# Norms by pairs of blocks behind the experts, a table loaded ahead, and products that nobody reads

## The chip, the cores and the metric

The kernel runs on one core of one Trainium2 chip. The core has five engines with queues of their own: TensorE (PE, with PEld for its weight loads), VectorE (DVE), ScalarE (ACT), GpSimd (POOL) and SyncE (SP, which here only issues DMAs). The metric is the device time of one execution in microseconds (us); a run gives one such time, and a median of several is compared. All numbers are float32.

## The reference

A two-layer perceiver: 16 sets of 64 tokens of 256 features (`x`, 1024 tokens, here 8 blocks of 128) read a memory `ctx` of 16 x 1601 rows. Six steps follow each other, each added to `x` after a layer norm:

```python
x = x + L0_xattn(_layernorm(x), ctx, top_k=32, ...)   # the 32 best of 1601 memory rows
x = x + L0_attn(_layernorm(x), ...)                   # retention with a decay
x = x + L0_ffn(_layernorm(x), ...)                    # attention over sets, then 8 experts
x = x + L1_xattn(_layernorm(x), ctx, ctx, ...)        # 16 heads over the whole memory
x = x + L1_attn(_layernorm(x), ...)                   # random features
x = x + L1_ffn(_layernorm(x), ...)                    # three trees of leaves, then attention
```

The places that matter here are the first norm with its queries, and the end of the third step with the norm that opens the fourth:

```python
def _ln(x, g, b, eps=1e-05):
    mu = jnp.mean(x, -1, keepdims=True)
    v = jnp.mean((x - mu) ** 2, -1, keepdims=True)
    return (x - mu) * jax.lax.rsqrt(v + eps) * g + b
# L0_ffn: each token goes to one expert, y is its gated output
y2 = _ln(y1 + moe(y1), ln2_g, ln2_b)
x = x + y2
# L1_xattn begins
qn = layernorm(_layernorm(x), norm_w, norm_b)
Q = qn @ Wq + bq
```

## The kernel before

`X` (128 partitions, 8 blocks, 256 features) stays on the core for the whole kernel. The blocks are handled in two halves of four. The program is written with tiles and a planner that puts the instructions of all engines in an order by modelled readiness and priority. Stages written under `manual_schedule` keep the written order on PE, DVE and ACT; the other queues (POOL, SP) are still ordered by the planner, and instructions outside such a stage are fitted in where the planner sees room. On each engine the order is then fixed: an instruction that waits holds up all behind it.

**The start (L475 to L490).** `normed_half(0)` takes the statistics of four blocks on DVE (`moments`, L152), a root on ACT (L160), a reciprocal (L161) and four normalised blocks `xn` (L280). `turned_half` turns them with PE transposes (L290) and copies them out by ACT and DVE (L293). `normed_half(1)` follows for the other half, then a small `power` activation that brings ACT the table of Exp (L479), then `queries(0)`: eight 128x512 products recorded at L211, which need the weights `w_x` from memory. The second half is turned, `query_keys(0)` makes the keys' side of the scores (L211 again, then L307), and `turned_and_scored` turns the first pair of memory tiles (L327) and scores them (L340). SP issues `X`, the first memory pair (L243, L246), then `rows` (L485) and further pairs; POOL issues `w_x`, `cols` and `w_mha`.

**The way back from the experts (L1179 to L1241).** Eight experts run one after the other on PE (L1098, L1112, L1115); ACT copies each result out (`ye`, L1117) and stores it to `done` in memory. While the results come back, PE and ACT also work on the memory of the next stage (values L632 and L640, turns L589 and L594): this filler is written earlier in the program with a lower priority, so the planner puts it where it finds room. `returned(k)` gathers block `k` of the results by an indirect DMA on POOL (L1182), adds it to `y1` with its gate (L1186), takes mean and variance (L1190, L1191), and leaves the centred, scaled block in `xa` (L1192). `root` is an activation with the square root on ACT (L1207) and a reciprocal on DVE (L1208). `summed(k)` adds the normed block to `X` (L1198) and takes the statistics of the sum (L1202, L1203). From these come `off` (L1223) and the normed queries `qn` (even blocks on DVE at L1233, odd ones on ACT at L1228). `turned_queries(0)` transposes them (L193, written out by ACT at L1155), and `head_pairs` makes the queries of all heads (L1165, L1173), after a `power` activation with Exp (L1238).

The order written before: an activation `root` on the constant `eps` (L1215), four `returned`, one root for the four, four `summed`, one root for the four, `off`, four `qn`, then the transposes; the second half's four `returned` come at the very end. `root` at L1215 depends only on `eps`; in the profiled execution it ran at 7.34 us, far ahead of its stage.

**What follows (L1696).** A loop over 16 sets, 4 parts and 2 column blocks: scores (`sc`, L1569), their maximum (`nmax`, L1582), exponents (L1590), transposes (L1604) and products with the values (L1624). In its first eight units a generator, `second_half`, finishes the second half: a root by Newton steps on POOL (`inverse_root`, L548 to L560), `summed` (L1198), POOL's `qn` (L1275), and `added` (L1252, L1259).

PSUM comes in pools with tags; tiles of one tag take turns: 5 buffers of tag `mm` at the start, 4 on the way back.

Of the kernel before, what the change touches and what calls it, by code (L numbers as in the profile page):

```python
# [10 lines left out]
F32 = mybir.dt.float32  # L11
I32 = mybir.dt.int32
AF = mybir.ActivationFunctionType
ALU = mybir.AluOpType
# [3 lines left out]
P = 128  # L18
D = 256
# [28 lines left out]
EPS = 1e-5  # L48
# [28 lines left out]
def perceiver_kernel(  # L77
# [178 lines left out]
    with ExitStack() as ph:  # L256
# [15 lines left out]
        qbk = act.tile([P, NB], F32, name="qbk", tag="qbk")  # L272
        qkTs = []

        def normed_half(half):
            xn = act.tile([P, NB // 2, D], F32, name="xn", tag=f"a{half}")
            k0, n = HALVES[half]
            mv, rstd = moments(X, k0, n)
            for k in range(n):
                nc.vector.tensor_scalar(  # L280
                    xn[:, k, :], X[:, k0 + k, :], mv[:, k, 0:1], rstd[:, k : k + 1],
                    ALU.subtract, ALU.mult,
                )
            return xn

        def turned_half(half, xn, copies):
            for c in range(2):
                pt = ps_m.tile([P, 512], F32, name="ps_t", tag="mm")
                for j in range(4):
                    nc.tensor.transpose(  # L290
                        pt[:, j * P : (j + 1) * P], xn[:, j, c * P : (c + 1) * P], ident
                    )
                copies[c](out=xnT[:, c, half * 512 : (half + 1) * 512], in_=pt)  # L293
# [179 lines left out]


        with tc.manual_schedule(engines=order):  # L475
            xn = normed_half(0)
            turned_half(0, xn, (nc.scalar.copy, nc.vector.tensor_copy))
            xn = normed_half(1)
            nc.scalar.activation(small.tile([P, 1], F32, name="power"), eps, AF.Exp)  # L479
            queries(0)  # L480
            turned_half(1, xn, (nc.vector.tensor_copy, nc.vector.tensor_copy))
            query_keys(0)
            mems = {0: pair(0)}
            sco = turned_and_scored(0, mems[0], nothing, nothing)
            nc.sync.dma_start(out=rows, in_=rows_in.partition_broadcast(P))  # L485
            mems[1] = pair(1)
            last = iter(())
            nc.gpsimd.tensor_tensor(
                X, X, row("L0_xattn_bo").unsqueeze(1).to_broadcast([P, NB, D]), ALU.add
            )  # L490
            for k in range(NB):
                chosen = []
                choice = choose(sco, chosen)
                next(last, None)
                next(choice)
                if k == 0:
                    queries(1)
                    query_keys(1)
                next(choice)
                next(last, None)  # L500
                next(choice)

                def between():
                    next(last, None)

                def behind():
                    next(choice, None)

                if k + 2 < NB:
                    mems[k + 2] = pair(k + 2)  # L510
                if k + 1 < NB:
                    sco = turned_and_scored(k + 1, mems[k + 1], between, behind)
                else:


                    cT = act.tile([P, 2, NT], F32, name="cT", tag="c")
                    taken = act.tile([P, NB // 2, D], F32, name="taken", tag="a0")
                    outputs(
                        0, lambda k, ps: nc.scalar.copy(taken[:, k : k + 2, :], ps), between
                    )  # L520
                    behind()
                    nc.vector.tensor_tensor(X[:, 0:4, :], X[:, 0:4, :], taken, ALU.add)
                last = gather(k, mems.pop(k), *chosen, k == NB - 2)
            for _ in last:
                pass
            outputs(1, lambda k, ps: nc.vector.tensor_tensor(
                X[:, k : k + 2, :], X[:, k : k + 2, :], ps, ALU.add
            ))
# [254 lines left out]
    with ExitStack() as ph:  # L783
# [395 lines left out]
        def returned(k, mv, dst):  # L1179

            back = qn[:, k, :]
            nc.gpsimd.indirect_dma_start(  # L1182
                out=back, out_offset=None, in_=done,
                in_offset=bass.IndirectOffsetOnAxis(ap=from_row[:, k : k + 1], axis=0),
            )
            nc.vector.scalar_tensor_tensor(  # L1186
                y1[:, k, :], back, gval[:, k : k + 1], y1[:, k, :], ALU.mult, ALU.add
            )
            st = small.tile([P, 6], F32, name="b_st", tag="b_st", bufs=2)
            nc.vector.bn_stats(out=st, in_=y1[:, k, :])  # L1190
            nc.vector.bn_aggr(out=mv, in_=st)  # L1191
            nc.vector.scalar_tensor_tensor(  # L1192
                dst, y1[:, k, :], mv[:, 0:1], row("ln2_g"), ALU.subtract, ALU.mult
            )
# [7 lines left out]
            nc.vector.bn_stats(out=st, in_=X[:, k, :])  # L1202
            nc.vector.bn_aggr(out=mv, in_=st)  # L1203

        def root(mv, scale, bias):
            rstd = small.tile([P, 4], F32, name="b_rstd", tag="b_rstd", bufs=2)
            nc.scalar.activation(rstd, mv[:, :, 1], AF.Sqrt, bias=bias, scale=scale)  # L1207
            nc.vector.reciprocal(rstd, rstd)  # L1208
            return rstd

        mvs = [small.tile([P, 4, 2], F32, name="b_mv", tag=f"b_mv{i}", bufs=1) for i in range(3)]
        with tc.manual_schedule(engines=order):
            nc.scalar.activation(small.tile([P, 1], F32, name="root"), eps, AF.Sqrt)  # L1215
            for k in range(4):
                returned(k, mvs[0][:, k, :], xa[:, k, :])
            rstd = root(mvs[0], 1.0, eps)
            for k in range(4):
                summed(k, xa[:, k, :], rstd[:, k : k + 1], mvs[1][:, k, :])  # L1220
            rstd = root(mvs[1], 1.0 + EPS, eps2)
            off = small.tile([P, 4], F32, name="b_off", tag="b_off", bufs=1)
            nc.vector.scalar_tensor_tensor(  # L1223
                off, mvs[1][:, :, 0], -1.0, rstd, ALU.mult, ALU.mult
            )
            for k in range(4):
                if k % 2:
                    nc.scalar.activation(  # L1228
                        qn[:, k, :], X[:, k, :], AF.Identity,
                        bias=off[:, k : k + 1], scale=rstd[:, k : k + 1],  # L1230
                    )
                else:
                    nc.vector.tensor_scalar(  # L1233
                        qn[:, k, :], X[:, k, :], mvs[1][:, k, 0:1], rstd[:, k : k + 1],
                        ALU.subtract, ALU.mult,
                    )
            turned_queries(0)
            nc.scalar.activation(small.tile([P, 1], F32, name="power"), eps, AF.Exp)  # L1238
            for oc in range(2):
                head_pairs(oc, 0)  # L1240
            for k in range(4, NB):  # L1241
                returned(k, mvs[2][:, k - 4, :], place[:, k - 4, :])
# [839 lines left out]
```

## Time and profile before

| what | value |
|---|---|
| median of 3 runs | 1519.57 us (1512.68 to 1520.9) |
| the profiled execution: its own time | 1511.88 us |
| its span | 1509.8 us |
| PE busy | 1457.7 us (97%), 10966 products |
| PEld / DVE / ACT / POOL busy | 65% / 66% / 52% / 21% |
| mean granted clock of TensorE | 0.992 |
| chain that ended last | PE 86%, DVE 7%, DMA 2%, issue 2%, POOL 1%, ACT 1% |

The span runs from the first to the last instruction that the profiler saw; the execution's own time has 2.1 us around it. "Busy" is time in which an engine's instructions ran; a busy PE is not PE at its peak, since products are pipelined and one f32 product leaves more than one record. The chain that ended last is followed back from the last instruction, at each step to what released it. The granted clock is the share of TensorE's full speed that it was allowed in a window. In a timeline the number in brackets is the idle time before a group and what ended it.

### The profile page before, as it was taken

Reading aid. Unit: us, or ns where it says so; the run is one execution under the profiler, and the core shown is the slowest. Engines: PE = TensorE matmul, PEld = TensorE weight load, DVE = VectorE, ACT = ScalarE, POOL = GpSimd, SP = SyncE. Lnnn points to the kernel's source line nnn. Section 1 sums busy time; section 2 is a strip of 40 time slices with the busy share of each in tenths; the row PEclk is TensorE's granted clock in tenths of the full one; section 3 lists DMA queues with packets and bytes.
Section 4 is the critical chain, followed back from the end, with each engine's and each line's share of the span. In section 5 each row is a group of like instructions: output and inputs, shape, how many; then the busy total and the mean of one; then the engine's idle time right before and its main releaser. Section 6 shows DMA issues by size and latency. Waiting matters only on the chain.

```text
span 1509.8 us, 28072 instructions
## 1 busy us (share of the span) xinstructions
PE 1457.7 (97%) x10966; PEld 988.6 (65%) x10966; DVE 995.2 (66%) x2111; ACT 788.3 (52%) x1983; POOL 320.3 (21%) x788
## 2 busy tenths in 40 slices
PE   7999988999979999999999999999999998999999
PEld 4666646677846777777777777777777665446445
DVE  2888858861268877877787787778776666523322
ACT  4666523341056666666666666666666565321221
POOL 2000007211032223132212313231240322231000
PEclk9999999999989999999999999999999999999999
DMA  9455132035621011011011101101110120100000
GB/s 327 144 168 168 37 115 72 1 126 181 221 76 45 3 45 47 4 46 45 11 39 45 46 3 47 45 15 35 45 45 3 45 88 10 37 1 0 0 14 14
DMA packets 76596, 92.85 MB, mean 62 GB/s; under 512 B 2584, under 2 KB 71760, under 8 KB 76336
## 3 DMA queue, kind: packets, MB, share of 16 engines
q1 hardware_dynamic: 72912, 82.82, 17.2%
q0 software_dynamic: 2400, 7.20, 1.9%
q8 instruction: 86, 1.41, 0.4%
q10 hardware_dynamic: 1152, 1.05, 0.2%
q14 instruction: 46, 0.38, 0.1%
HBM read 85.82 MB, written 5.24 MB: 60 GB/s over the span
## 4 chain that ended last, share of the span: by engine, by line
PE 86%; DVE 7%; DMA 2%; issue 2%; POOL 1%; ACT 1%; SPq 0%; DVEq 0%; POOLq 0%; ACTq 0%
PE ps_v L632 12%; PE ps_k L610 11%; PE pt L1604 9%; PE sc L1569 7%; PE po L1624 7%; PE ps_h L1834 5%; PE ps_o L1856 4%; PE pt L327 3%; PE sc L340 3%; DVE nmax L1582 3%; PE pu L412 3%; PE pt L589 3%; PE ps_p L211 2%; PE ps_h L1098 2%; PE ps_v L1868 2%; PE ps_y L1112 2%
## 5 line engine op out<-in xcount | busy, mean ns | idle before, releaser
L1590 ACT ACTIVATE a<-sc,nmax 128x384 f32<-128x384 f32 (+2 forms) x512 | 304.4, 600 | 162.8 <-DVE nmax L1582 162.8
L1582 DVE TENSOR_REDUCE nmax<-sc 128x1 f32<-128x384 f32 (+2 forms) x512 | 258.2, 567 | 97.0 <-PE sc L1569 96.9
L1604 PEld LDWEIGHTS pt<-ident,a 128*128 128x128 f32 (+1 forms) x1664 | 189.3, 141 | 47.2 <-issue 26.7
L1612 DVE COPY aT<-pt 128x512 f32<-128x512 f32 (+1 forms) x288 | 191.4, 686 | 34.5 <-PE pt L1604 26.3
L632 PE MATMUL ps_v<-w_x,mT 128*128 128x256 f32 (+1 forms) x832 | 202.6, 382 | 2.9 <-ACT kT L618 1.0
L610 PE MATMUL ps_k<-mT,w_x 128*128 128x384 f32 (+2 forms) x512 | 204.7, 523 | 0.5 <-ACT kT L618 0.5
L1604 PE MATMUL pt<-ident,a 128*128 128x128 f32 (+1 forms) x1664 | 204.6, 274 | 0.0
L632 PEld LDWEIGHTS ps_v<-w_x,mT 128*128 128x128 f32 (+1 forms) x832 | 145.6, 186 | 25.4 <-DVE aT L1612 5.1
L610 PEld LDWEIGHTS ps_k<-mT,w_x 128*128 128x128 f32 x512 | 87.0, 189 | 103.9 <-issue 72.1
L1569 PE MATMUL sc<-kT,qh 32*128 32x384 f32 (+2 forms) x1024 | 124.1, 547 | 0.0
L1624 PE MATMUL po<-aT,v 128*32 128x128 f32 (+1 forms) x3328 | 118.3, 277 | 6.0 <-DVE aT L1612 6.0
L594 ACT ACTIVATE mT<-pt,cols 128x384 f32<-128x384 f32 (+2 forms) x128 | 87.0, 683 | 63.2 <-PE pt L589 62.3
L576 POOL TENSOR_SCALAR memt<-memt,m_nmean,m_rstd 128x256 f32<-128x256 f32 (+1 forms) x208 | 113.0, 560 | 1.7
L1590 ACT ACTIVATION_READ_ACCUMULATOR a<-sc,nmax 128x1 f32 x512 | 105.9, 207 | 0.0
L1624 PEld LDWEIGHTS po<-aT,v 128*32 128x32 f32 (+1 forms) x3328 | 82.5, 109 | 31.6 <-issue 14.2
L618 ACT ACTIVATE kT<-ps_k,cols 128x384 f32<-128x384 f32 (+2 forms) x128 | 75.9, 594 | 35.4 <-PE ps_k L610 34.5
L570 DVE BATCH_NORM_STATS2 m_st<-memt 128x6 f32<-128x256 f32 (+1 forms) x208 | 83.7, 403 | 6.9 <-DMA memt<-in_mem_dram 6.6
L640 DVE COPY v<-ps_v 128x512 f32<-128x512 f32 (+1 forms) x112 | 64.9, 580 | 35.3 <-PE po L1624 28.0
L1609 ACT COPY aT<-pt 128x512 f32<-128x512 f32 x128 | 75.6, 591 | 0.7 <-PE pt L1604 0.7
L1823 DVE SCALAR_TENSOR_TENSOR hT<-leafb,memt,hT 128x512 f32<-128x512 f32 x48 | 35.2, 747 | 57.2 <-ACT hT L1841 57.2
L589 PE MATMUL pt<-ident,memt 128*128 128x128 f32 (+1 forms) x416 | 67.1, 273 | 5.7 <-ACT mT L594 1.7
L1841 ACT ACTIVATE hT<-ps_h,cols 128x512 f32<-128x512 f32 x48 | 33.0, 687 | 74.9 <-PE ps_h L1834 74.9
(369 smaller groups left out, 2000.8 us busy)
## 6 DMA issues: line engine op xcount, KB each, us to landing
memt<-in_mem_dram SPq DMA_DIRECT2D x32, 1536.0 KB
w<-in_moe_w_dram SPq DMA_DIRECT2D x16, 1024.0 KB
memt<-in_mem_dram SPq DMA_DIRECT2D x32, 65.0 KB
w_x<-in_w_x_dram POOLq DMA_DIRECT2D x2, 1024.0 KB
mT<-in_fff_w_dram SPq DMA_DIRECT2D x2, 1024.0 KB
kT<-in_fff_w_dram SPq DMA_DIRECT2D x2, 1024.0 KB
rows<-in_rows_dram SPq DMA_DIRECT2D x1, 1430.5 KB
X<-in_x_dram SPq DMA_DIRECT2D x2, 512.0 KB
```

What stands on the lines that cost most here:

```text
L570: nc.vector.bn_stats(out=st[0:m, c, :], in_=mt[0:m, c, :])
L576: nc.gpsimd.tensor_scalar(mt[0:m, c, :], mt[0:m, c, :], nmean[0:m, c : c + 1], rstd[0:m, c : c + 1], ALU.add, ALU.mult,)
L589: nc.tensor.transpose(pt[:, j * P : j * P + chunk(c)], mt[0 : chunk(c), c, dc * P : (dc + 1) * P], ident[0 : chunk(c), 0 : chunk(c)],)
L594: nc.scalar.activation(mT[:, dc, c0 * P : c0 * P + n], pt[:, 0:n], AF.Identity, bias=col("L1_norm_b", dc), scale=col("L1_norm_w", dc),)
L610: nc.tensor.matmul(ps[:, 0:n], lhsT=wk[:, dc, oc * P : (oc + 1) * P], rhs=mT[:, dc, n0 : n0 + n], start=(dc == 0), stop=(dc == 1),)
L632: nc.tensor.matmul(ps[0 : chunk(c), j, :], lhsT=mT[:, dc, c * P : c * P + chunk(c)], rhs=wv[:, dc, :], start=(dc == 0), stop=(dc == 1),)
L1569: nc.tensor.matmul(scs[j][:, 0:n], lhsT=qh[rs, oc, b, :, :], rhs=kT[rs, oc, c0 * P : c0 * P + n], start=True, stop=True,)
L1582: nc.vector.reduce_max(out=nm, in_=sc[:, 0:n], axis=AX.X, negate=True)
L1590: nc.scalar.activation(aj[:, 0:n], sc[:, 0:n], AF.Exp, bias=nm, accum_out=tot[:, blk, part : part + 1])
L1604: nc.tensor.transpose(pt[0:m, j * P : (j + 1) * P], a[j][:, c * P : c * P + m], ident)
L1612: nc.vector.tensor_copy(aT[0:m, :], pt[0:m, :])
L1624: nc.tensor.matmul(po[32 * j : 32 * j + 32, :], lhsT=v[0:m, c0 + c, blk * 32 : (blk + 1) * 32], rhs=aTs[c][0:m, j * P : (j + 1) * P], star ...
```

## The change

At the start two groups of products of the identity with itself are issued on PE, 16 ahead of everything and 8 between the first half's transposes and the queries. They write a PSUM tile that nobody reads. On the way back the first half's four blocks go by pairs: the first pair's root is taken while the third block comes back, the second norm's root of the first pair while the fourth does, and the third and fourth blocks are summed after the first pair's queries are normed. Each root is now an activation of two columns, and its reciprocal stands where its result is used. The activation `root` at the head of the stage reads `even` (written on DVE at L1132 to L1134, at the end of the experts) in place of `eps`. Eight products of the identity with the fourth returned block, 128x256 each, go to PE ahead of the transposes; nobody reads them either.

```diff
+        def awake(n):
+            ps = ps_m.tile([P, P], F32, name="ps_w", tag="mm")
+            for _ in range(n):
+                nc.tensor.matmul(ps, lhsT=ident, rhs=ident, start=True, stop=True)
...
         with tc.manual_schedule(engines=order):
+            awake(16)
             xn = normed_half(0)
             turned_half(0, xn, (nc.scalar.copy, nc.vector.tensor_copy))
+            awake(8)
             xn = normed_half(1)
...
-        def root(mv, scale, bias):
-            rstd = small.tile([P, 4], F32, name="b_rstd", tag="b_rstd", bufs=2)
+        def root(mv, scale, bias, i):
+            rstd = small.tile([P, 2], F32, name="b_rstd", tag=f"b_rstd{i}", bufs=2)
             nc.scalar.activation(rstd, mv[:, :, 1], AF.Sqrt, bias=bias, scale=scale)
+            return rstd
+
+        def normed_pair(k, rstd):
             nc.vector.reciprocal(rstd, rstd)
-            return rstd
+            off = small.tile([P, 2], F32, name="b_off", tag="b_off", bufs=2)
+            nc.vector.scalar_tensor_tensor(
+                off, mvs[1][:, k : k + 2, 0], -1.0, rstd, ALU.mult, ALU.mult
+            )
+            nc.vector.tensor_scalar(
+                qn[:, k, :], X[:, k, :], mvs[1][:, k, 0:1], rstd[:, 0:1],
+                ALU.subtract, ALU.mult,
+            )
+            nc.scalar.activation(
+                qn[:, k + 1, :], X[:, k + 1, :], AF.Identity,
+                bias=off[:, 1:2], scale=rstd[:, 1:2],
+            )
...
         with tc.manual_schedule(engines=order):
-            nc.scalar.activation(small.tile([P, 1], F32, name="root"), eps, AF.Sqrt)
-            for k in range(4):
-                returned(k, mvs[0][:, k, :], xa[:, k, :])
-            rstd = root(mvs[0], 1.0, eps)
-            for k in range(4):
-                summed(k, xa[:, k, :], rstd[:, k : k + 1], mvs[1][:, k, :])
-            rstd = root(mvs[1], 1.0 + EPS, eps2)
...
+            nc.scalar.activation(small.tile([P, 1], F32, name="root"), even, AF.Sqrt)
+
+            returned(0, mvs[0][:, 0, :], xa[:, 0, :])
+            returned(1, mvs[0][:, 1, :], xa[:, 1, :])
+            first = root(mvs[0][:, 0:2, :], 1.0, eps, 0)
+            returned(2, mvs[0][:, 2, :], xa[:, 2, :])
+            nc.vector.reciprocal(first, first)
+            for k in range(2):
+                summed(k, xa[:, k, :], first[:, k : k + 1], mvs[1][:, k, :])
+            second = root(mvs[1][:, 0:2, :], 1.0 + EPS, eps2, 1)
+            returned(3, mvs[0][:, 3, :], xa[:, 3, :])
+            ps = ps_m.tile([P, D], F32, name="ps_w", tag="mm")
+            for _ in range(8):
+                nc.tensor.matmul(ps, lhsT=ident, rhs=xa[:, 3, :], start=True, stop=True)
+            first = root(mvs[0][:, 2:4, :], 1.0, eps, 0)
+            normed_pair(0, second)
+            nc.vector.reciprocal(first, first)
+            for k in range(2, 4):
+                summed(k, xa[:, k, :], first[:, k - 2 : k - 1], mvs[1][:, k, :])
+            second = root(mvs[1][:, 2:4, :], 1.0 + EPS, eps2, 1)
+            normed_pair(2, second)
             turned_queries(0)
```

More of the change, by code (lines that the diff above doesn't have):

```diff
@@ L1222, in perceiver_kernel @@
[L1222 to L1236, printed above, removed]
+            nc.scalar.activation(small.tile([P, 1], F32, name="root"), even, AF.Sqrt)
```

## The prediction

> **What bounds the kernel now.** I read the share of each engine first (PE 97%, DVE 66%, ACT 52%), then the chain of waits that ended last (PE 86%, DVE 7%), in order of time at the two places that the change touches, then the windows of the granted clock there. The chain at the start:
>
> ```profile
> 1.63 10.38 DMA w_x<-in_w_x_dram
> 12.02 0.14 issue
> 12.15 6.20 PE ps_p L211 x8
> 18.34 0.87 PE ps_t L290 x8
> 19.22 3.44 PE ps_p L211 x8
> 22.66 1.68 PE ps_b L307 x16
> 24.33 3.55 PE pt L327 x32
> ```
>
> Columns: start, length, what. From 12.15 us on TensorE never waits, so what it loses is lost at the end. Two groups of eight 128x512 products (L211) are alike, and the first takes 6.20 us, the second 3.44: until 17.2 us each record takes 0.85 us, then 0.43. The chain on the way back from the experts:
>
> ```profile
> 430.10 0.67 ACT mT L594
> ...
> 430.79 1.28 ACT L1207
> 432.09 0.31 ACT b_rstd L1207
> ...
> 436.98 0.31 ACT b_rstd L1207
> ...
> 438.19 2.04 PE ps_t L193 x8
> 440.25 5.50 PE ps_q L1165 x8
> 445.75 1.11 PE sc L1569 x8
> 446.86 2.47 DVE nmax L1582 x4
> 449.32 0.41 DVE X L1198
> ```
>
> The fourth block's variance is ready at 428.99 us, but ScalarE is in an evacuation of `mT` and must then load the square root's table (1.28 us): VectorE idles 2.85 us (429.57 to 432.42). Then come four blocks in a row on VectorE, a second root, and PE at half speed: L193 takes 0.255 us a transpose (0.115 at full clock: L327, 32 in 3.69 us), L1165 0.85 us a record at first. The clock, in windows of 3.41 us (PE busy, PEld, DVE, ACT, POOL, then granted clock):
>
> ```profile
> 351.70:355.12 3.42, 3.42 (x17) 3.14 (x16) 1.25 (x2) 0.64 (x2) 0.00 (x0) 0.51 0.00 0
> 355.12:358.53 3.41, 3.41 (x30) 3.36 (x30) 1.02 (x2) 0.00 (x0) 0.00 (x0) 0.99 0.00 0
> 426.80:430.21 3.41, 1.56 (x10) 0.85 (x9) 2.59 (x7) 1.18 (x3) 2.65 (x3) 1.00 0.41 109
> 430.21:433.62 3.41, 1.12 (x4) 0.72 (x4) 1.10 (x4) 3.38 (x5) 0.00 (x0) 0.51 0.31 68
> 437.04:440.45 3.41, 2.24 (x9) 1.59 (x10) 2.96 (x9) 2.28 (x5) 0.00 (x0) 0.50 0.39 123
> 440.45:443.86 3.41, 3.41 (x5) 1.35 (x6) 3.17 (x10) 2.09 (x3) 0.00 (x0) 0.50 0.01 2
> 443.86:447.28 3.42, 3.42 (x15) 1.38 (x14) 1.36 (x4) 2.89 (x4) 2.11 (x10) 0.99 0.02 5
> ```
>
> All changes of the clock in this execution fall on one grid of 3.41 us. A window with PE 46% busy (1.56 us) is followed by half clock, one with 63% (2.15 us, at 1235.75) is not; from half clock a full window lifts it, one with 66% (2.24 us) does not.
>
> **The start: unread products.** `ident` is ready at 1.47 us, TensorE's first real work at 8.24 us, so `awake(16)` has 6.7 us of idle time. A 128x128 f32 product leaves two records (L1098: 16 products, 32 records in 3.84 us, 0.12 each at full clock), so 32 records, about 0.24 each at half clock (L193's 0.255 the nearest row). They fill the window to 6.96 us; by then some 22 are done, the other 10 take 1.2 us: end at 8.1, before the first `xn` is out (8.09 + wait = 8.24). With other grids they end by 8.9, and the transposes, now 0.115 each, still end by 9.8. `awake(8)` is 16 records, 9.75 to 11.6, under the wait for `w_x` (12.02 us). The windows 6.96 to 10.37 and 10.37 to 13.79 then hold some 2.4 and 2.8 us, above the 2.15 that held the clock. So the first L211 group costs 3.44 instead of 6.20. What is late next: the second half's `xn`, at 15.3 us before, 0.5 earlier now, since VectorE's copy at 10.48 waited for the slow transposes; PE needs it at 15.59. ScalarE's `qT` copies end at 15.3 and 16.55, keys start at 16.46 and need the second only 0.86 us later. L327 would start at 12.15 + 3.44 + 0.87 + 3.44 + 1.68 = 21.6 instead of 24.33: **2.7 us**. Its cover is thin: the second tile of the first memory pair is needed at 22.5. `rows` (1430.5 KB) stands behind it on SP's queue and had landed at 25.91; at 418 GB/s, the most in any 2 us there, it takes 3.5 us, so the pair was there by 22.4. Bounds: 0 (it lands only at 24.33, where the trace proves it) to 2.8.
>
> [...]
>
> **The way back.** *Table.* The root's first use moves from L1215's cheap place at 7.34 us (0.19 us, off the chain) to behind `even`, which is written at 413.77 to 414.24. ScalarE then idles 7.48 us until the last `ye` copy (417.21), which hides 1.28 + 0.20; without that cover 1.48 would go before the last expert's store. No Exp stands between there and the roots, so the load at 430.79 goes.
>
> *VectorE by pairs.* A returned block costs 1.60 us, a summed one 1.06, a reciprocal or `off` 0.21, a `qn` block 0.33. From 423.05: blocks 0 to 2 end at 427.84. The first root's data are there at 425.81, its 0.30 us lies under block 2. Reciprocal and two sums: 430.2. The second root lies under block 3, which ends at 431.8 (its gather stays fourth on POOL, issued 424.04, landing 2.83 later like the first, so 426.9; all eight gathers leave POOL by 430.1 as before). Reciprocal, `off`, `qn` 0: 432.6; the third root was ready under block 3. Reciprocal and two sums: 434.95. The fourth root isn't hidden: 0.36. Reciprocal, `off`, `qn` 2: 436.1, where block 4 starts; before, 438.38. So 2.85 of idling leaves, three more small instructions (0.63) come, 2.3 remain. Block 7's variance then is ready at 442.0, POOL's root (4.43 us, 444.43 to 448.86 before) done at 446.6.
>
> *PE.* The 8 unread products of 128x256 are 16 records (L632: 32 in 7.17 us, 0.22), waiting for `xa` 3 at 431.8. The clock has fallen by then (430.21), so at 0.43: unless 82% busy lifts it at 433.62, it rises at 437.04 after 12 records, the rest end at 437.9. Queued behind them: the transposes, whose input is ready at 436.3, so 1.6 us are given back; L193 then takes 0.95 instead of 2.04, L1165 3.44 instead of 5.50. ScalarE: two `qnT` to 440.1, Exp's table and `power` to 441.6, two `qh` to 443.1. The first scores start there instead of 445.68; `nmax` ends at 446.75. That meets POOL's root: summed block 4 (L1198) starts at 446.75 instead of 449.24, **2.5 us**, and from there all follows in the old order. If the clock rises at 433.62, scores come at 441.1, but POOL's root still ends at 446.6: nothing more. If it never rises, 443.9 and 0.8 us less. Bounds: -1.0 (first rival) to 2.9 (all idling gone).
>
> **Sum.** 2.7 + 2.5 = 5.2 us. The profiled execution took 1511.88 us (span 1509.8, 2.1 around it): 1506.7. It and the fastest run (1512.68) lie 8 us below the other two (1519.57, 1520.9); nothing in the page tells why, though the grid's phase differs from run to run at most by some us. I put the gain on the middle of the four, 1516.1, and predict **1511 us**.
>
> **Rivals.**
> 1. *ScalarE's queue hides no root.* The four waiting evacuations (L594) are interleaved with roots by the planner. If the first root stands behind the one at 430.10, which itself waits for PE, the reciprocal comes at 431.15 instead of 427.84, 3.3 us late, and the way back loses 1.0. For it: the old first root stood exactly there. Against: its data come 3.2 us earlier, when only three evacuations are done. 2.7 - 1.0 = 1.7: 1514.4. Chance 0.15.
> 2. *Transposes don't hold the clock.* Window 6.96 to 10.37 then counts 1.4 us (42%, under the 46% that fell): half clock at 10.37, `awake(8)` ends at 12.6, the clock is back at 13.79, and the start gains 1.7, not 2.7: 1512.0. Against: 64.98 to 68.40 is 2.96 us transposes of 3.42 and stayed at 1.00; 351.70 to 355.12 has 1.97 us of them and lifted. [...] 0.05.
> 3. *First memory pair late.* Start gains nothing: 2.5, 1513.6. 0.10.
> 4. *Slower: the unread products don't lift the clock.* Products of one identity may not count as work like others. Then `awake(8)` runs 10.4 to 14.1, past 12.15, and the first queries end 0.75 later than now; on the way back 16 x 0.43 end at 438.7, the transposes 0.6 later. Together +1.35: 1517.5. It decides from the point where 32 products leave the clock at half at 8.24. Against: busy share alone explains every window above. 0.08.
> 5. *More than forecast*: the two half-clock windows that cost most elsewhere (187.87 and 464.34 lead into them, up to 1.7 us each) fall away as the work shifts: 8.6, 1507.5. 0.10.
>
> **How the numbers follow.** Forecast 0.52. The range 1502.5 to 1518.5 takes the sum on the lower pair of executions with rival 5 below (1512 - 8.6 = 1503.4) and the sum of rival 1 on the upper pair (1520 - 1.7 = 1518.3). 0.5%, 7.6 us, is about what a measurement of this kernel can tell from no change. 1511 against 1519.57 is 0.56%, but the new median may fall in the lower pair (1507, 0.8%) or the upper (1515, 0.3%), the former likelier if the phase of the clock made the upper one: within the forecast 0.6 to 0.4; rival 5 is mostly faster, rivals 1 to 3 a third, rival 4 same or slower. Together faster 0.50, same 0.40, slower 0.10.
>
> **What would show it.** Right: L211's first group near 3.5 us, L327 at 21.6, no idle before it from `memt`; no table load at the first root, one near 414; VectorE idle under 0.5 us in all from 423 to the second summed pair; L1165 near 3.5; summed block 4 some 5 us earlier than 449.3. Wrong: L211 still at 0.85 a record, a root that waits behind L594, or `pt` L327 waiting for a DMA. The prediction falls if the end moves by less than 2 us or more than 9.

## The result and the profile after

The changed kernel took 1509.71 us (median of 21 runs, 1505.43 to 1516.35), the kernel before 1520.52 us beside it (21 runs, 1511.95 to 1521.59). The ratio on record is 0.9945, with a 95% interval of 0.9931 to 0.9958; it is not the quotient of the two medians, which is 0.993. The profiled execution took 1505.43 us, span 1503.6, mean granted clock 0.995, 6.45 us less than the one profiled before.

The times of both kernels fall into two groups. Before: 4 runs at 1512 and 17 from 1518.6 to 1521.6. After: 19 from 1505.4 to 1511.0 and 2 at 1515.5 and 1516.4. The gain in the median therefore has two parts: within the short group some 3.6 us (medians 1512.2 and 1508.6; both profiles belong to it), and a shift from the long group to the short one. The start and the way back can be read in the two profiles. The second part needed experiments of its own.

The start, TensorE's timeline of the changed kernel. Columns: start, length, engine, line, what, and in brackets the idle time before it with what ended it.

```profile
1.53 6.39 PE L280 MATMUL ps_w<-ident 128*128 128x128 f32 x32 [1.53 <-POOL eps L135]
...
9.85 1.95 PE L280 MATMUL ps_w<-ident 128*128 128x128 f32 x16
12.21 3.67 PE L211 MATMUL ps_p<-xnT,w_x 128*128 128x512 f32 x8 [0.41 <-DMA w_x<-in_w_x_dram]
...
16.59 3.60 PE L211 MATMUL ps_p<-qT,w_x 128*128 128x512 f32 x8
...
21.73 3.69 PE L334 MATMUL pt<-ident,memt 128*128 128x128 f32 x32
```

L280 is `awake`; L334 was L327. The first group of L211 takes 3.67 us instead of 6.20, the two groups are now alike, and the memory's transposes start at 21.73 instead of 24.20 (this view's start of the group, 24.33 in the chain) without waiting for the memory: 2.47 us won. The granted clock reads 1.00 from 6.96 to 13.79 us in both profiles, so the speed there is told by the instructions' times alone.

The way back, the timeline of the changed kernel with ScalarE's lines and one of VectorE's (L1217 is the root, L603 was L594):

```profile
414.75 1.28 ACT L1240 ACT_TABLE_LOAD   x1
...
419.88 0.30 ACT L1217 ACTIVATE b_rstd<-b_mv,eps 128x2 f32<-128x2 f32 x1 [0.38 <-issue]
...
425.67 1.45 ACT L603 ACTIVATE mT<-pt,cols 128x512 f32<-128x512 f32 x2 [0.77 <-PE pt L598]
427.01 0.47 ACT L1217 ACTIVATE b_rstd<-b_mv,eps 128x2 f32<-128x2 f32 x2
427.33 0.17 DVE L1221 RECIPROCAL b_rstd<-b_rstd 128x2 f32<-128x2 f32 x1 [1.47 <-ACT b_rstd L1217]
```

The table is loaded ahead and the first root is hidden, as forecast. The second root had its data at 424.3 us, but stood in ScalarE's order behind two evacuations that themselves waited for TensorE, until 427.01. The last line shows the price, 1.47 us of VectorE's time.

TensorE's timeline (L1253 are the unread products, L1174 was L1165):

```profile
425.92 5.81 PE L1253 MATMUL ps_w<-xa,ident 128*128 128x256 f32 x16
431.56 1.10 PE L193 MATMUL ps_t<-ident,qn 128*128 128x128 f32 x8
433.09 3.70 PE L1174 MATMUL ps_q<-qnT,w_x 128*128 128x512 f32 x8 [0.43 <-ACT qnT L1164]
```

The products are over at 431.73, before ScalarE has written the last `qn` block (431.84), so they hold up little, and the real ones run at full clock (granted 1.00 in the window from 430.19 to 433.60; L1174 takes 3.70 us, L1165 5.50 before). But the chain of waits reaches the fifth summed block (L1207, was L1198) through GpSimd's root, not through the scores:

```profile
441.74 0.21 POOL c_rstd L567
441.97 0.49 DVE X L1207
```

Between the last `ye` copy and that block lie 30.61 us (411.36 to 441.97), against 32.03 before (417.21 to 449.24): 1.42 us won, not 2.5. The other 3.4 us of the 5.85 by which the last `ye` came earlier were won between 22 and 411 us, where the code is the same: the wait for the memory ahead of its statistics, at 217 us, fell from 2.29 to 1.17 us, and the window at 351.7 was not one of half clock (granted 1.00, before 0.51). The shorter wait goes with the start: it is 1.2 to 1.5 us in all eight profiles with unread work there, in the runs below too, and 2.3 to 2.5 in the six without. The windows of the changed kernel (columns as in the prediction):

```profile
419.95:423.36 3.41, 1.69 (x11) 0.93 (x9) 3.20 (x10) 2.50 (x5) 2.50 (x4) 1.00 0.37 106
423.36:426.77 3.41, 2.93 (x10) 2.20 (x11) 2.33 (x7) 1.86 (x4) 1.08 (x1) 0.50 0.31 77
...
443.84:447.25 3.41, 1.12 (x8) 0.86 (x7) 3.41 (x7) 2.91 (x8) 0.00 (x0) 1.00 0.00 0
447.25:450.66 3.41, 3.41 (x20) 2.30 (x23) 3.10 (x10) 0.37 (x2) 0.00 (x0) 0.50 0.00 0
```

The window with TensorE 50% busy (419.95) is followed by one of half clock (0.50). The pause at 446 us (2.29 us) now fills most of one window (33% busy), and 447.25 to 450.66 runs at half clock: `ps_n` there (L1276) takes 3.33 us instead of 1.99. The sixth and the seventh summed block lie 7.03 us apart (448.89 to 455.92) instead of 5.40 (456.17 to 461.57), so 1.6 us of the gain is lost again.

### The profile page after: what moved, and what is told of

It reads as the page before. It is cut to its first block, busy times and chain, and to the rows that moved or that the text cites. A ratio compares the mean times of both kernels' runs of the same rounds, so it can differ in the third digit from the quotient of the medians.

```text
span 1503.6 us, 28202 instructions
## 1 busy us (share of the span) xinstructions
PE 1464.3 (97%) x11030; PEld 997.1 (66%) x11030; DVE 995.4 (66%) x2114; ACT 789.2 (52%) x1985; POOL 322.8 (21%) x788
## 4 chain that ended last, share of the span: by engine, by line
PE 63%; DVE 6%; POOL 1%; issue 1%; ACT 0%; POOLq 0%; DVEq 0%; ACTq 0%
PE ps_v L641 11%; PE ps_k L619 10%; PE pt L1628 9%; PE sc L1593 7%; PE po L1648 7%; PE ps_h L1858 5%; PE ps_o L1880 3%; DVE nmax L1606 3%; PE pt L598 2%; PE ps_v L1892 2%; DVE aT L1636 1%; PE ps L1431 1%; PE pt L1682 1%; PE pf L1464 1%; PE pf L1469 1%
## 5 line engine op out<-in xcount | busy, mean ns | idle before, releaser
L603 ACT ACTIVATE mT<-pt,cols 128x384 f32<-128x384 f32 (+2 forms) x128 | 87.1, 684 | 62.9 <-PE pt L598 61.9
```

Source lines behind the costliest of these rows:

```text
L603: nc.scalar.activation(mT[:, dc, c0 * P : c0 * P + n], pt[:, 0:n], AF.Identity, bias=col("L1_norm_b", dc), scale=col("L1_norm_w", dc),)
```

## The experiments

All results, with the way back measured as above (last `ye` copy to the fifth summed block, of the profiled execution). Kernels of one block ran on one chip; each block has its own runs of the kernel before. The ratios are those on record and, like the one above, not quotients of medians.

| kernel | median, us | range (runs) | ratio [95%] | way back, us |
|---|---|---|---|---|
| before, beside the next four | 1512.02 | 1506.09 to 1518.23 (30) | | |
| e1_start | 1504.45 | 1502.49 to 1507.03 (10) | 0.9949 [0.9925, 0.9972] | 29.4 |
| e2_back | 1511.99 | 1504.88 to 1521.44 (12) | 0.9998 [0.9971, 1.0024] | 29.1 |
| e3_noprod | 1503.62 | 1502.48 to 1515.93 (9) | 0.9954 [0.9928, 0.9981] | 30.0 |
| e4_eps | 1503.66 | 1500.92 to 1513.35 (12) | 0.9949 [0.9924, 0.9974] | 29.1 |
| before, beside the next four, one execution | 1520.07 | | | |
| b1_before, one execution | 1521.48 | | | 32.4 |
| b2_before, one execution | 1512.02 | | | 32.4 |
| e5_turns, one execution | 1509.46 | | | 32.0 |
| e6_first, one execution | 1505.42 | | | 31.7 |
| before, beside the next four | 1512.68 | 1510.19 to 1521.92 (34) | | |
| f1_pieces | 1513.26 | 1509.85 to 1514.69 (12) | 0.998 [0.9959, 1.0] | 32.0 |
| f2_early | 1513.51 | 1511.67 to 1522.74 (12) | 0.9994 [0.997, 1.0019] | 31.8 |
| f3_both | 1507.35 | 1504.15 to 1511.02 (11) | 0.9941 [0.9918, 0.9963] | 31.2 |
| f4_again | 1507.79 | 1505.17 to 1516.84 (12) | 0.9949 [0.9926, 0.9972] | 31.9 |

**The two halves of the change, one at a time.** e1_start has the products at the start and the old way back:

```diff
+            awake(16)
             xn = normed_half(0)
...
+            awake(8)
             xn = normed_half(1)
```

> Only the start of the change: the 16 and 8 unread products, the way back as before. Theory A (the forecast's sum): L211's first group takes 3.4 to 3.7 us instead of 6.2, the first transposes of memory start 2.5 us earlier, the span is 2.5 us shorter than before's 1509.8 and the median 2.5 us below 1520.5. Theory B: the start also decides where the windows of half clock fall later (in the changed kernel the windows at 351.7 and 467.8 were gone), so the last expert's evacuation comes 5 to 6 us earlier than 417.2, as in the changed kernel, and the median falls by 5 us or more. Theory C: the 3.4 us that the changed kernel won between 22 and 411 us beyond the start are chance of one execution; then the last expert's evacuation is 2.5 to 3.5 us earlier.

e2_back has the new way back and no `awake`:

```diff
-            awake(16)
...
-            awake(8)
```

> Only the way back of the change: pairs, the table ahead and the 8 products, without products at the start. Theory A: from the last expert's evacuation to the second half's first sum 30.6 us instead of 32.0, as in the changed kernel (1.4 us won), median 1.4 to 2.5 us below before. Theory B (windows of half clock decide): the way back is as short as that, but the median moves by another amount, between no gain and 5 us, as windows fall elsewhere.

Measured: the start alone has the whole gain in the median (0.9949). The way back alone has none that the times can show: 0.9998, with an interval of about 0.26% or 4 us to either side. The profiles are finer. In seven of the eight profiled executions with the old order (all but e1_start) VectorE idles 2.85 to 3.60 us ahead of the first reciprocal, and the way back takes 31.7 to 32.4 us. In e1_start it takes 29.4. The timeline of e1_start there, ScalarE's and VectorE's lines:

```profile
422.24 3.84 ACT L601 ACTIVATE mT<-pt,cols 128x384 f32<-128x384 f32 x6
426.10 1.28 ACT L1214 ACT_TABLE_LOAD   x1
...
427.72 0.18 DVE L1215 RECIPROCAL b_rstd<-b_rstd 128x4 f32<-128x4 f32 x1 [0.28 <-ACT b_rstd L1214]
```

Here the six evacuations ran through without a wait for TensorE, and the table's load, at the same place as ever, was over when VectorE had its fourth variance. So the stall is made by evacuations that stand still, and the 1.28 us of the load count only behind them. The new order has the same two cases. In e2_back, e3_noprod and e4_eps the evacuations ran through, no root was late, and the way back took 29.1 to 30.0 us; in the changed kernel, f3_both and f4_again they stood, the second root was late by 1.47, 1.96 and 2.56 us, and it took 30.6 to 31.9. The mean of the old order's eight is 31.7, of the new order's six 30.3, a difference of 1.4 us. But most of it comes from how often each case occurred. Like with like, the new order is 0.8 us shorter where the evacuations stood (means 31.2 of three and 32.0 of seven) and 0.35 us where they ran through (29.1 in e2_back and e4_eps, which have the products, against 29.4 in e1_start). Three of six against one of eight is too few to say that the new order lets them run through more often. All of this is too little for the medians. What held TensorE's transposes ahead of those evacuations isn't shown: their waits are put down to "issue" (1.5 us before) or to ScalarE's own evacuation.

One more thing shows in e1_start: the first memory pair was late there. TensorE's timeline:

```profile
23.68 4.47 PE L332 MATMUL pt<-ident,memt 128*128 128x128 f32 x24 [0.97 <-DMA memt<-in_mem_dram]
```

It waited 0.97 us, and 24 transposes took 4.47 us after that; at the 0.115 each of the changed kernel (32 in 3.69) they would take 2.76. Nothing of the start's gain was left: the next group of L211 begins at 36.21 us, in the kernel before at 35.94. So the prediction's third rival came true in this execution, though not in the others. The last `ye` copy still came 2.43 us earlier (414.78 against 417.21): 1.0 us was won in the wait for the memory at 217 us, the rest behind 254 us (there the copy of `xaT` was 0.83 us earlier, 254.18 against 255.01). So what the changed kernel won beyond the start is not chance of one execution (theory C). The median of the ten executions is 7.6 us below the kernel before beside it, as theory B has it, since none of them falls in the long group.

**Two parts of the way back.** e3_noprod is the changed kernel without the eight unread products on the way back:

```diff
-            ps = ps_m.tile([P, D], F32, name="ps_w", tag="mm")
-            for _ in range(8):
-                nc.tensor.matmul(ps, lhsT=ident, rhs=xa[:, 3, :], start=True, stop=True)
```

> The changed kernel without the 8 unread products on the way back. Theory A (the forecast: VectorE and POOL's root set the second half's first sum, PE is not on that path): half clock lasts from 423.4 to the end of a full window near 434 to 437, the transposes and the first queries take 2.0 and 5.5 us again, yet the second half's first sum is late by no more than 0.8 us against the changed kernel; median within 1 us of its 1509.7. Theory B: the products pay for themselves, and without them the median is 2 us or more above 1509.7.

e4_eps lets the first real root load the table again:

```diff
-            nc.scalar.activation(small.tile([P, 1], F32, name="root"), even, AF.Sqrt)
+            nc.scalar.activation(small.tile([P, 1], F32, name="root"), eps, AF.Sqrt)
```

> The changed kernel with the activation before the stage reading eps again, so that it runs at 7 us and the root's table is loaded at the first root. Theory A: the load of 1.28 us at the first root, whose data are there near 419.9, is nearly hidden: the reciprocal at 421.9 has 1.6 us of block 2 before it, so the loss is 0 to 0.3 us and the evacuations behind it move by 1.3. Theory B: the load pushes ScalarE's evacuations and with them the second root, which was already 1.5 us late; the way back loses the full 1.3 us, median 1511.

Neither part is worth anything that the times can show: both kernels, each without it, have the ratio of the start alone. But in e3_noprod TensorE does pay. Its chain of waits:

```profile
430.62 6.11 PE ps_q L1174 x8
...
440.31 0.40 DVE X L1207
```

L1174 takes 6.11 us instead of 3.70, so the products do make the queries faster. The chain now reaches the fifth summed block through the queries and their scores: GpSimd's root was over at 439.30, and the block began at 440.23, 30.0 us after the last `ye` copy. That is no later than in the changed kernel (30.6), as theory A has it, but there the evacuations stood. Where they ran through and the products were there (e2_back, e4_eps), it comes after 29.1 us. By this comparison the eight products are worth 0.9 us when no evacuation stands, and theory A's reason, that TensorE is not on that path, holds only with them. In e4_eps ScalarE loads the table at 420.20, ahead of the first real root; the reciprocal behind that root comes without a wait, and the way back takes 29.1 us.

**What makes an execution long.** The kernel before was profiled twice more, beside two variants of the start, to see whether the long executions differ at the start or elsewhere.

> The kernel before, unaltered, profiled again. Its executions spread from 1506 to 1518 us with the mean granted clock between 0.995 and 0.990. Theory A: the start makes the difference: where the grid of 3.41 us windows falls so that the window with the keys' small products (L307) or the first queries is not full, half clock lasts from the start well past 17.2 us, up to the scores of the first pair near 36, and the first pair ends 5 us or more later than in the first profile. Theory B: the start is as before within 2 us, and a long execution has more windows of half clock elsewhere (near 190, 350, 430, 465), each worth 1 to 2 us.

> The same kernel once more, for another phase of the grid. Theories and numbers as for the first repetition; if the two differ by 5 us or more, the stretch in which they part tells which theory holds.

e5_turns takes twice as many transposes in place of the products (with the old way back), e6_first only the sixteen:

```diff
-                nc.tensor.matmul(ps, lhsT=ident, rhs=ident, start=True, stop=True)
+                nc.tensor.transpose(ps, ident, ident)
```

> The start's unread products replaced by as many unread transposes of the identity (32 and 16 records, the way back as before). Theory A (transposes count as work for the clock, as the window 64.98 to 68.40 of the kernel before suggests): L211's first group takes 3.4 to 3.7 us as with products. [...]

> Only the first 16 unread products at the start, not the 8 under the wait for w_x. The window from about 7.0 to 10.4 holds some 1.8 us of work, the next, to 13.8, some 1.7 us (50%), with a grid as in the first profile. Theory A (a window with under about half its time in work is followed by half clock): the clock falls at 10.4 or 13.8 in this or a shifted grid and L211's first group takes 4.5 to 6.5 us. Theory B (once lifted the clock stays until a nearly idle window): 3.4 to 3.7 us, and the 8 products are worth nothing.

e5_turns: the first group of L211 takes 3.67 us too, against 6.20 in the kernel before, so the transposes of an identity did here what the products do. e6_first: 3.67 us again without the eight, whose place under the wait for `w_x` needs no filling here.

By luck b1_before was a long execution and b2_before a short one of the same kernel on the same chip. They agree to within a microsecond until 220 us, so theory A, the start, is out; the last `ye` copy is at 417.7 in b2 and at 426.4 in b1. The first difference is a half-clock window at 237.88 in b1 (granted 0.50, and TensorE 53% busy in the window before it). What follows is worth reading line by line. The timeline of b1_before from 254 to 262 us, all engines:

```profile
254.59 5.40 DVE L911 TENSOR_TENSOR xa<-xa,rows 128x256 f32<-128x256 f32 x3
...
254.75 4.62 POOL L937 TENSOR_TENSOR X<-X,rows 128x2048 f32<-128x2048 f32 x1 [0.55 <-DVE xa L182]
...
256.63 1.12 PE L211 MATMUL ps_p<-xaT,w_mha 128*128 128x512 f32 x2
259.91 1.00 DVE L150 COPY xaT<-ps_t 128x512 f32<-128x512 f32 x1
...
260.97 1.31 PE L211 MATMUL ps_p<-xaT,w_mha 128*128 128x512 f32 x2 [3.22 <-DVE xaT L150]
```

The same stretch in the execution profiled before:

```profile
255.01 1.02 DVE L150 COPY xaT<-ps_t 128x512 f32<-128x512 f32 x1
255.26 4.51 POOL L937 TENSOR_TENSOR X<-X,rows 128x2048 f32<-128x2048 f32 x1
...
255.88 4.50 DVE L911 TENSOR_TENSOR xa<-xa,rows 128x256 f32<-128x256 f32 x2
```

GpSimd adds a row to all of X in one instruction of 4.5 us (L937). While it ran, VectorE's additions (L911) stood still: the two beside it took 4.50 us here, the three ahead of it 1.19, and in b1_before three took 5.40 us beside it and two 0.73 behind it, which leaves 4.7 for one. In the short execution VectorE's copy of `xaT`, which TensorE waits for, gets ahead by 0.25 us and the stall falls on additions that nobody needs soon. In the long one the slow window had delayed VectorE, GpSimd was already waiting for X and began at once, and the copy stood behind a stalled addition: 259.91 instead of 255.01. TensorE waited 3.22 us, was 24% busy in that window, and the next (261.78) ran at half clock (0.50).

**Testing that trap.** The trap is this order: GpSimd's long addition begins before VectorE's are through, and the copy of `xaT` stands behind both. f1_pieces cuts the addition, in the kernel before:

```diff
-        nc.gpsimd.tensor_tensor(
-            X, X, row("ln2_b").unsqueeze(1).to_broadcast([P, NB, D]), ALU.add
-        )
+        for k in range(NB):
+            nc.gpsimd.tensor_tensor(X[:, k, :], X[:, k, :], row("ln2_b"), ALU.add)
```

> The kernel before, with GpSimd's addition of the bias row to X (128x2048, one instruction of 4.5 us) cut into eight of 128x256. Theory A, a trap: in the long execution of the kernel before the addition began 0.16 us after VectorE's first addition of a row to xa and ahead of the copy of xaT, that VectorE addition stood until GpSimd was done, the copy behind it began at 259.9 instead of 255.1, and TensorE waited 3.2 us, which made the next window one of half clock. By A the eight pieces let VectorE in between: the copy is never more than about 1 us late, no execution goes over about 1515, and the median is 1509 to 1512, ratio about 0.993 where the kernel before mostly runs at 1519 to 1521, and 0.997 to 1.000 where it mostly runs at 1512. Theory B, many places: the long executions come from windows of half clock that fall at many places with the phase of their grid, and the addition is only one of them; then the times spread as those of the kernel before, up to 1518 and more, ratio 0.998 to 1.002.

Twelve runs, none over 1514.69, where 15 of the 34 of the kernel before on that chip were between 1520.18 and 1521.92. In f1's profile the window at 238 is slow as well (0.50), and the addition begins first. The same timeline of f1_pieces:

```profile
254.42 6.51 POOL L938 TENSOR_TENSOR X<-X,rows 128x256 f32<-128x256 f32 x8
...
255.25 2.68 DVE L911 TENSOR_TENSOR xa<-xa,rows 128x256 f32<-128x256 f32 x3
...
257.85 1.00 DVE L150 COPY xaT<-ps_t 128x512 f32<-128x512 f32 x1
...
258.91 3.27 PE L211 MATMUL ps_p<-xaT,w_mha 128*128 128x512 f32 x7 [0.91 <-DVE xaT L150]
```

VectorE gets in between the pieces: three additions in 2.68 us instead of 5.40, TensorE waits 0.91 us instead of 3.22, and the next slow window comes only at 354.33. The numbers expected were too good: the copy comes 2.8 us after that of the short execution (257.85 against 255.01), not 1, and the median (1513.26) is not below the short group of the kernel before, because an execution with the slow window at 238 but without the trap, like the profiled one (1514.56), is still longer than that group.

f2_early tried to force the trap by making GpSimd ready sooner:

```diff
-        nc.gpsimd.dma_start(out=wg, in_=w_gate.rearrange("(c p) e -> p c e", p=P))
+        nc.sync.dma_start(out=wg, in_=w_gate.rearrange("(c p) e -> p c e", p=P))
...
-        nc.gpsimd.memset(zero, 0.0)
+        nc.vector.memset(zero, 0.0)
```

> The kernel before, with GpSimd relieved of 1.1 us of work ahead of the addition (the gate's weights are issued by SyncE, the zeros are set by VectorE), so that the addition begins as soon as X is free. Theory A: it begins near 254.2, before VectorE's three additions of the second half are through, the copy of xaT comes only at about 258.7, TensorE waits some 3 us there, a window of half clock follows, and nearly all executions are long, 1515 to 1522, with ratio 1.003 to 1.007 where the kernel before mostly runs at 1512 and 1.000 where it mostly runs at 1520. Theory B: the median is that of the kernel before within 0.1 per cent, and short executions are as frequent as there.

That missed. Five of twelve runs were long (1518.9 and more), as often as in the kernel before. The profiled one was long, and its lines are those of b1_before: the window at 238.58 slow (0.50), the addition at 254.86, the copy at 260.02, TensorE waiting 3.23 us, half clock at 262.48 (0.50). So in every profile with the trap, and in f1, the slow window near 238 came first; a readier GpSimd alone did not make it more frequent. No short execution of f2 was profiled, so where its addition stood there is open. f1 and f2, both with the slow window, give the price of the trap: ScalarE's fourth copy of `qT` (L236) begins at 265.22 and at 269.08, 3.9 us apart. At the last `ye` copy they are 5.6 us apart (419.9 and 425.5), because f2 has two windows of half clock from 358.05 where f1 has one at 354.33; whether the trap brought on the second isn't shown. The kernel before without the window at 238 had that copy at 417.2; 8.3 us in all is about what separates its two groups (medians 1512.1 and 1520.75 of the 34 runs).

f3_both is the changed kernel with the pieces, f4_again the changed kernel itself:

> The changed kernel with the addition in eight pieces. Theory A: no execution over 1511, median 1503 to 1508, as the changed kernel without its long ones; it is then 3 to 6 us better than the kernel before in pieces (2.5 us of the start and what the windows do). Theory B: the changed kernel's median and spread, some executions at 1515.

> The changed kernel again, as the measure for the other three on this chip. Both theories: 1504 to 1510 with one execution in ten near 1516. By theory A the profile of an execution near 1516 has the copy of xaT behind the addition; by either theory one under 1510 has it ahead.

f3_both has no run over 1511.02 and a median of 1507.35, f4_again one of twelve at 1516.84 and 1507.79: the medians are the same within their spread, and one long run in twelve is too few to say that the pieces cure it. Against the kernel before with the pieces, the changed kernel with them is 5.9 us shorter (1513.26 to 1507.35), which is the change without the trap on either side. The start's 2.5 us, the 1.1 us of the memory's wait and 0.8 us of the way back (32.0 to 31.2) make 4.4 of it; the rest isn't traced.

## Why the prediction was right, and where it was not

The time was met (1511 forecast, 1509.71 measured, in the range), but the sum behind it was right in one of its two terms, and the rest came from where the prediction had nothing. That the two numbers lie so close is partly luck. 1511 is 1516.1 less 5.2, and 1516.1 is a level between the two groups at which the kernel before has no run. Measured, the medians lie 10.8 us apart: 3.6 us within the short group, and a shift between the groups that the prediction didn't have in its sum.

- **The start, 2.7 us: right.** 2.47 measured, by the steps given: `awake(16)` over at 7.92 (8.1 forecast), `awake(8)` from 9.85 to 11.8, L211 3.67 (3.44 forecast, from the chain's view), the transposes at 21.73 (21.6 forecast, where the chain's view has 24.33 before and the timeline 24.20). The eight were not needed (e6_first).
- **First memory pair late (rival 3):** not in the changed kernel's profile, but once in e1_start, at 0.97 us of waiting and 24 transposes in 4.47 us, which took the whole gain. The bounds that the prediction gave (0 to 2.8) were the right ones.
- **Transposes don't hold the clock (rival 2):** refuted by e5_turns (L211 3.67 us, as with products). Its sum was off too: by the prediction's own times the window 6.96 to 10.37 holds 1.8 us of products (1.2 from 6.96, 0.6 from 9.75), not 1.4; 1.49 was measured. **Unread products don't lift it (rival 4):** refuted at the start by 3.67 against 6.20 us, and on the way back by 3.70 against 6.11 us. The argument against it, that busy share alone explains every window, holds for the profile from which it was read and not for later ones (see the last section).
- **The way back, 2.5 us: wrong in size.** 1.42 us in the two profiles, 0.35 to 0.8 between profiles of the same case, not visible in the medians. The step that failed is "The second root lies under block 3": where the evacuations stand it comes 1.47 to 2.56 us late. GpSimd's root, forecast to be done at 446.6 in the times of the kernel before, was done at 447.8 in them (441.95, with the last `ye` copy 5.85 us earlier), and the block waited for it. That is the first rival's mechanism on the second root instead of the first; its price was put at 1.0 us of loss, and the runs show a smaller gain instead. The 2.85 us of idling that were to leave are real in seven of eight executions of the old order, but they come from standing evacuations, of which the new order keeps a part; the table's load ahead is worth nothing that shows (e4_eps).
- **PE on the way back:** in the times of the kernel before (5.85 us later than in the profile) the clock fell at 429.2, not at 430.21, the products ran from 431.8, as forecast, and were over at 437.6 instead of 437.9, and the transposes lost next to nothing to them. All this is covered by GpSimd's root, as the prediction said that it would be for an earlier clock.
- **"From there all follows in the old order":** not quite; the pause at 446 us met the grid and cost 1.6 us.
- **More than forecast (rival 5):** half right. Of the two slow windows that it named, the one at 467.8 fell away and the one at 191.3 moved to 187.8. One that it didn't name, at 351.7, fell away as well, and one at 447.25 is new.
- **The level:** the prediction said that nothing in the page tells why two of the four times lay 8 us lower, and took the middle. The runs show why: the trap at 254 us, 3.9 us or more, after a slow window at 238. The changed kernel falls into the long group more rarely. Counting runs some 8 us above the shortest group, kernels with the products at the start and the addition whole had 6 of 64 (the changed kernel's two sets, e1_start, e3_noprod and e4_eps), kernels without them 49 of 97 (the kernel before's three sets and e2_back). That the long runs of the other kernels are the same trap is inferred from their length; only two long executions were profiled.

What stays open: why the products at the start make the trap rarer. They move the work at 254 us by 1 to 5 us against the grid, but the grid's phase differs between executions, and the pause near 234 us is as deep with them as without: TensorE is 53% busy in the 3.41 us from 234.10 in the first profile (1.80 us) and in e1_start (1.82), and 56% in the worst such stretch of the changed kernel (from 230.30). In three profiles with them the copy was 0.94 us ahead of the addition rather than 0.25, in five others again 0.25. Both may matter; no run here separates them. Nor was it traced how the products at the start shorten the wait for the memory at 217 us (1.1 us).

## What to carry to other kernels

Unread products are worth their place where TensorE is idle ahead of work that bounds the kernel: sixteen of them at the start moved everything behind by 2.5 us, while on the way back, where another engine's chain is nearly as long, the same device bought 0.9 us at most by one comparison of profiles, and nothing that the times show. Moving an instruction away from a queue that stands still helps only if the ones behind it aren't put into the same queue again: here one late root became another. When a kernel's times form two groups, profile one of each and look for the first difference; a long GpSimd instruction that holds up VectorE is a cheap thing to cut into pieces (here 6.51 us in eight instead of 4.62 in one, and TensorE's wait 0.91 us instead of 3.22).

## What the runs showed of the hardware

The changes of the granted clock lie whole periods of 3.41 us apart in the executions read for it: 191.32, 351.70, 430.21 and 467.79 us in the first profile (47, 70 and 81 periods from the first), 190.49 and 354.33 in f1_pieces (48), 238.58, 262.48 and 358.05 in f2_early (7 and 35). The phase of this grid differs between executions: in b1_before, the same kernel as in the first profile, the slow window from 237.88 lies 13.64 periods behind 191.32, while the work (the end of TensorE's pause of 1.20 us there) was 0.62 us earlier (235.79 against 236.41).

One slow window brought on another in b1_before. The one at 237.88 (0.50) delayed VectorE into the trap; the pause of 3.22 us there left TensorE 24% busy in the window from 258.37 (0.81 us), and the next ran at half clock (0.50).

Neither the longest pause in a window nor its busy share told for certain what followed. A window 53% busy (1.80 us) without a pause over 1.2 us was followed by half clock (b1_before, 234.47). And the same pause of 1.90 us ahead of the same products (`po`), in a window 44% busy (1.51 us), was followed by half clock in the first profile (from 464.38) and by a granted clock of 1.00 in that of the changed kernel (from 457.48).
